# Cross-attention on one core: product 4 of the block product y in smaller blocks, sums of half 0 by accumulating DMA, result 12 evicted ahead of inner sums

## The chip, the cores and the metric

The kernel runs on one core of a Trainium2 chip. The metric is device time in microseconds (us) of one execution. A core has five engines with a queue of instructions each: PE (TensorE, matrix products into PSUM), DVE (VectorE), ACT (ScalarE), POOL (GpSimd) and SP (here a queue that issues DMAs). They meet through semaphores. Sixteen DMA engines move data; SP, ACT and POOL issue transfers to them.

## The reference

For each of 8 batches, with x1 and x2 of 512 x 1024 (channels x positions), in f32:

```python
q = jnp.einsum('bcn,dc->bnd', x1, Wq) + bq        # Wq: 64 x 512
k = jnp.einsum('bcn,dc->bdn', x2, Wk) + bk[:, None]
v = jnp.einsum('bcn,dc->bdn', x2, Wv) + bv[:, None]
attn = jax.nn.softmax(jnp.einsum('bnd,bdm->bnm', q, k), axis=2)
attn_out = jnp.einsum('bcm,bnm->bcn', v, attn)
return attn_out + x1
```

## The kernel before, in words

The values are never formed: the kernel computes y = x2 times the transposed attention (512 x 1024 by 1024 x 1024), scales it by one over the sums of the softmax, and then out = Wv y + bv + x1.

Both large products are done by a scheme of Strassen's kind with seven block products in place of eight (`MULT`: 1, 2, 6, 7, 5, 3, 4, in the order of their use). `first(i)` is block product i of y, `second(i)` that of the output. The left blocks of y are `a["11"]` to `a["22"]`, loaded from x2 transposed, and their sums S1 to S4; the right blocks are quarters of the exponentials `e` and their sums T1 to T4, all made on VectorE. The PSUM banks "a" and "c" (two of 128x512 each: j = 0, 1) are chains into which several block products accumulate; what has to leave a chain midway is copied by ScalarE to tiles `uy1`, `uy6`, `uy5` (tags u10 to u61). `evict_y` and `evict_o` combine a bank with such a copy on VectorE: result 11 of y is bank c after product 2 plus the copy from product 1, 22 is c after 7 plus the copy from 5, 12 is bank a after 3, 21 is c after 4 plus the copy from 6 (`RESULT`). Each result of y is then multiplied by `rden`, one over the softmax's sums.

A softmax half is 512 of the 1024 query positions (h = 0, 1), held as `e[h]` of 128 x 2 x 4 x 512. For each half: `scores` (PE) and copies to SBUF (ACT); `fold` and `fold_halves` of the maxima (DVE); `highest`, an all-reduce over the partitions (POOL); `exponentials`, a subtraction (DVE) and an exponential (ACT) for each of four slices; `sums`, three folds of 128x1024 and, in `total`, a fold of the two halves (DVE), an all-reduce (POOL) and a small DMA `few<-den`; `shares`, a reciprocal (DVE) and two DMAs on POOL's queue, `row<-few` to DRAM and the broadcast `den<-row` back.

`period(s, n, nn, nnn)` is the order of one batch s, written out by hand; nothing reorders it. It also makes the scores and exponentials of the next batch n, the queries of the one after it and loads. So every engine's queue is in the order of this program. Tiles come from pools with a tag and a number of buffers; a new tile waits until the old one of its buffer has been read.

Product 2 of y is already split once more, in batches 1 to 7: `inner_left` and `inner_right` make four sums each of the quarters of A12 and of the right block 21, `multiply_inner` issues seven products of 128x128 by 128x256 with two steps each, and `evict_inner` puts result 11 together on VectorE. In before, product 4 is one whole block product (`first(4)`: eight matmuls of 128x128 by 128x512); the sums of half 0 of the next batch are folded by VectorE just after the second scores, and `shares(n, 0)` follows the maxima of half 1.

An f32 matmul stands in the trace as two records.

Of the kernel before, what the change touches and what calls it, by code (L numbers as in the profile page):

```python
# [15 lines left out]
def kernel(  # L16
# [8 lines left out]
    bv: bass.AP,  # L25
    out: bass.AP,
):

# [187 lines left out]

    def total(s, h):
        fold_halves(s, h, ALU.add)  # L220
        s.den[h] = sb.tile([P, H], F32, tag="den", name=f"den_{s.b}_{h}", bufs=3)
        nc.gpsimd.partition_all_reduce(s.den[h], s.mx[h][:, 0, :], P, ReduceOp.add)  # L222
        s.few[h] = sb.tile([P, H // P], F32, tag="few", name=f"few_{s.b}_{h}", bufs=2)
        nc.gpsimd.dma_start(
            s.few[h], s.den[h][0:1, :].rearrange("o (p f) -> o p f", p=P)
        )
# [80 lines left out]
                s.tmp[i, j] = sb.tile([P, H], F32, tag=f"u{i}{j}", name=f"u{stage}{i}{j}_{s.b}")  # L307
                nc.scalar.copy(s.tmp[i, j], ps)  # L308

    def inner_left(s):  # L310

        x = s.a["12"]
        v = {
            f"{p + 1}{q + 1}": x[:, ts(q, MH // 2), ts(p, P)] for p in range(2) for q in range(2)
        }
        sums = sb.tile([P, 4, MH // 2, P], F32, tag="aS4", name=f"aI_{s.b}")
        for i, (k, x, y, op) in enumerate(
            (
                ("S1", "21", "22", ALU.add),
                ("S2", "S1", "11", ALU.subtract),  # L320
                ("S3", "11", "21", ALU.subtract),
                ("S4", "12", "S2", ALU.subtract),
            )
        ):
            v[k] = sums[:, i]
            nc.vector.tensor_tensor(v[k], v[x], v[y], op)
        s.inner["a"] = v

    def inner_right(s):

        x = s.e[0][:, 1]
        v = {
            f"{q + 1}{r + 1}": x[:, ts(q, MH // 2), ts(r, H // 2)]
            for q in range(2)
            for r in range(2)
        }
        sums = sb.tile([P, 4, MH // 2, H // 2], F32, tag="eT4", name=f"eI_{s.b}")
        for i, k in enumerate(("T1", "T2", "T3", "T4")):
            v[k] = sums[:, i]
            x, y = {"T1": ("12", "11"), "T2": ("22", "T1"), "T3": ("22", "12"), "T4": ("21", "T2")}[k]  # L340
            nc.vector.tensor_tensor(v[k], v[x], v[y], ALU.subtract)
        s.inner["t"] = v

    def multiply_inner(s):


        a, t = s.inner["a"], s.inner["t"]
        half = [P, H // 2]
        chain = ps_a.tile(half, F32, tag="c0", name=f"ps_i0_{s.b}")
        second = ps_a.tile(half, F32, tag="c1", name=f"ps_i1_{s.b}")  # L350
        third = ps_s.tile([P, 2, H], F32, tag="sc", name=f"ps_i2_{s.b}")[:, 0, 0 : H // 2]
        u = sb.tile([P, 2, H // 2], F32, tag="u50", name=f"i6_{s.b}")
        w = sb.tile([P, 2, H // 2], F32, tag="u51", name=f"i1_{s.b}")
        for i, ps, copy in (
            (1, chain, w[:, 0, :]),
            (2, second, None),
            (6, chain, u[:, 0, :]),
            (7, third, w[:, 1, :]),
            (5, chain, u[:, 1, :]),
            (4, third, None),  # L360
            (3, chain, None),
        ):
            ka, kb, _, _ = MULT[i]
            for k in range(MH // 2):
                nc.tensor.matmul(  # L365
                    ps,
                    a[ka][:, k, :],
                    t[kb][:, k, :],
                    start=i in (1, 2, 7) and k == 0,
                    stop=i in (2, 3, 4) and k == MH // 2 - 1,  # L370
                    skip_group_check=True,
                )
            if copy is not None:
                nc.scalar.copy(copy, ps)
        s.inner["ps"] = chain, second, third
        s.inner["u"] = u, w

    def evict_inner(s):

        chain, second, third = s.inner["ps"]  # L380
        u, w = s.inner["u"]
        u0, u1 = s.tmp[1, 0], s.tmp[1, 1]
        left, right = slice(0, H // 2), slice(H // 2, H)
        s.y["11"] = y = sb.tile([P, 2, H], F32, tag="y11", name=f"y11_{s.b}")
        for out, x, z in (
            (u0[:, left], u0[:, left], w[:, 0, :]),
            (y[:, 0, left], second, u0[:, left]),
            (u1, u1, u.rearrange("p a n -> p (a n)")),
            (y[:, 1, right], w[:, 1, :], u1[:, right]),
            (y[:, 1, left], third, u1[:, left]),  # L390
            (y[:, 0, right], chain, u0[:, right]),
        ):
            nc.vector.tensor_tensor(out, x, z, ALU.add)


    RESULT = {"11": ("c", 1), "22": ("c", 5), "12": ("a", None), "21": ("c", 6)}
# [26 lines left out]
    def evict_o(s, k):  # L423
        bank, add = RESULT[k]
        for j in range(2):
            c = 2 * (int(k[0]) - 1) + j
            o = s.o[k, j]
            nc.vector.scalar_tensor_tensor(  # L428
                o, s.bank[bank, j], bv_sb[:, c : c + 1], o, ALU.add, ALU.add
            )  # L430
        for j in range(2):
            c, h = 2 * (int(k[0]) - 1) + j, int(k[1]) - 1
            o = s.o[k, j]
            if add is not None:
                nc.vector.tensor_tensor(o, o, s.tmp[add, j], ALU.add)
            nc.sync.dma_start(out[s.b, ts(c, P), ts(h, H)], o)

    def sums(s, h):
        for i in range(1, MH):
# [95 lines left out]
    def period(s, n, nn, nnn):  # L535

        def first(i):
            multiply(s, "y", i, s.a, s.t, MH)  # L540

        def second(i):
            multiply(s, "o", i, w, s.y, 2)

        open_t(s)
        first(1)
        if s.b == 0:
            head_second(s, n)
        sum_e(s, "T1", "T2")
        if s.b == 0:  # L550
            total(s, 0)
        if n:
            load_a(n, "11")
        if s.b == 0:
            first(2)
            evict_y(s, "11", (1,))
            keys(n)
            load_x(nn, x1)
            sum_t4(s)
            sums(s, 1)  # L560
            shares(s, 0)
        else:
            multiply_inner(s)
            sums(s, 1)
            evict_inner(s)
            sum_t4(s)
            sum_a(s, "S4")
        sum_e(s, "T3")
        if n:
            load_a(n, "12", "21", "22")  # L570
        first(6)

        def next_queries():
            queries(nn)
            load_x(nn, x2)

        def next_keys():
            keys(nn)
            if nnn:
                load_x(nnn, x1)  # L580

        if n:
            scores_and(n, 0, "c", next_queries if nn else nothing)
            for i in range(1, MH):
                fold(n, 0, i, "max", ALU.max)
            highest(n, 0)
        shares(s, 1)
        evict_y(s, "11", (2,))
        first(5)
        fetch_o(s, "11")  # L590
        fetch_o(s, "22")
        if n:
            for i in range(MH):
                exponentials(n, 0, i)
            if s.b:
                sum_a(n, "S1", "S2", "S3")
        first(7)
        evict_y(s, "22")
        first(3)
        evict_y(s, "12")  # L600
        if n:
            scores_and(n, 1, "a", next_keys if nn else nothing)
            sums(n, 0)
        sum_y(s, "T1")
        sum_y(s, "T2")
        if n:
            if s.b:
                inner_left(n)
            else:
                left_sums(w, "S1", "S2", "S3", "S4")  # L610
            for i in range(1, MH):
                fold(n, 1, i, "max", ALU.max)
            highest(n, 1)
            shares(n, 0)
        first(4)
        evict_y(s, "21")
        second(1)
        sum_y(s, "T3")
        sum_y(s, "T4")
        second(6)  # L620
        fetch_o(s, "12")
        if n:
            exponentials(n, 1, 0)
            exponentials(n, 1, 1)
        second(2)
        evict_o(s, "11")
        fetch_o(s, "21")
        second(5)
        if n:
            exponentials(n, 1, 2)  # L630
            exponentials(n, 1, 3)
        second(7)
        evict_o(s, "22")
        if s.b == 0:
            sum_a(n, "S1", "S2")
        elif n:
            inner_right(n)
        if n:
            second(3)
            evict_o(s, "12")  # L640
            second(4)
            evict_o(s, "21")
            if s.b == 0:
                sum_a(n, "S3")
                inner_left(n)
                inner_right(n)
        else:
            second(4)
            evict_o(s, "21")
            second(3)  # L650
            evict_o(s, "12")
# [37 lines left out]
```

## Time and profile before

| what | value |
|---|---|
| median of 3 runs | 712.3 us (711.54 to 714.22) |
| the profiled execution | 711.94 us |
| its span, first to last instruction | 710.2 us |
| PE busy | 700.5 us, 1976 records |
| VectorE busy | 576.9 us |
| ScalarE busy | 210.7 us |
| POOL busy | 118.4 us |
| DMA moved | 91.67 MB, 129 GB/s on average |

A line of the page's groups reads: source line, engine, operation, tiles written and read, shape, count, then busy time in all, mean ns of one, and the idle time of the engine just before them with what ended it. A line of the timeline or of the chain begins with its start and its length in us. Engines are named PE, DVE, ACT, POOL; PEld is PE's load of weights.

### The profile page before, as it was taken

The page shows a single profiled execution, that of the slowest core. Times are in us where ns is not written, and L with a number is a line of the kernel's source. Part 1 is how long each engine was busy: PE and PEld are TensorE (multiplying, and loading weights), DVE is VectorE, ACT ScalarE, POOL GpSimd, SP SyncE. Part 2 cuts the span into 40 slices and gives each one's busy share as a digit, 9 for nine tenths or more (in the row PEclk, how much of TensorE's full clock was granted, in tenths as well). Part 3 has the DMA queues.
Part 4 walks back from the last instruction along what each step waited for, and adds up shares of the span by engine and source line. Part 5 has one row for each costly group of instructions (what it writes and reads, how often), then busy time and mean ns, then how long its engine had stood idle before and what let it go on. Part 6 is the DMA issues. An engine that isn't in the chain of part 4 may idle for free.

```text
span 710.2 us, 5772 instructions
## 1 busy us (share of the span) xinstructions
PE 700.5 (99%) x1976; PEld 315.8 (44%) x1976; DVE 576.9 (81%) x653; ACT 210.7 (30%) x299; POOL 118.4 (17%) x86
## 2 busy tenths in 40 slices
PE   8999999999999999999999999999999999999997
PEld 4333444534445434454344543454434544445443
DVE  0998698997989869888798887898788988999154
ACT  2733423144221522224221332413324134231010
POOL 0123130120402112021210212102121020402000
PEclk9999999999999999999999999999999999999999
DMA  9567333163431714327143362332702350042003
GB/s 327 221 227 255 111 148 134 60 198 99 161 121 61 257 37 163 149 82 244 37 147 128 119 208 90 123 128 89 237 0 74 119 178 16 5 167 80 15 0 148
DMA packets 37005, 91.67 MB, mean 129 GB/s; under 512 B 5232, under 2 KB 5232, under 8 KB 36976
## 3 DMA queue, kind: packets, MB, share of 16 engines
q1 hardware_dynamic: 33344, 84.95, 33.9%
q0 software_dynamic: 2368, 4.27, 2.8%
q10 hardware_dynamic: 1264, 2.10, 1.0%
q8 instruction: 15, 0.25, 0.2%
q14 instruction: 14, 0.11, 0.0%
HBM read 72.62 MB, written 16.81 MB: 126 GB/s over the span
## 4 chain that ended last, share of the span: by engine, by line
PE 85%; DVE 8%; DMA 4%; POOL 1%; issue 1%; ACT 1%; SPq 0%; DVEq 0%; ACTq 0%; POOLq 0%
PE ps_ya L298 25%; PE ps_oa L298 15%; PE ps_yc L298 15%; PE ps_oc L298 12%; PE ps_i L365 5%; PE ps_s L187 5%; PE ps_k L145 3%; PE ps_q L145 3%; DVE eT L251 2%; DMA x_head<-in_x_dram 1%; DVE e L245 1%; DMA row<-few 1%; PE ps_sa L187 1%; DVE sum L208 1%; DMA x_in_x_dram<-in_x_dram 1%; PE ps_sc L187 1%
## 5 line engine op out<-in xcount | busy, mean ns | idle before, releaser
L222 POOL PARTITION_ALL_REDUCE den<-sum x16 | 59.6, 3726 | 327.2 <-DVE sum L212 322.3
L298 PE MATMUL ps_ya<-eT,aS 128*128 128x512 f32 x256 | 113.1, 595 | 0.0
L308 ACT COPY uy<-ps_ya 128x512 f32<-128x512 f32 x48 | 28.0, 587 | 198.0 <-PE ps_ya L298 180.9
L298 PEld LDWEIGHTS ps_ya<-eT,aS 128*128 128x128 f32 x256 | 48.0, 190 | 60.9 <-issue 60.0
L245 DVE TENSOR_TENSOR e<-e,top 128x1024 f32<-128x1024 f32 x60 | 70.0, 1217 | 1.4 <-POOL top L217 1.4
L196 ACT COPY e<-ps_s 128x1024 f32<-128x1024 f32 x47 | 46.7, 1028 | 69.5 <-PE ps_s L187 67.2
L308 ACT COPY uo<-ps_oa 128x512 f32<-128x512 f32 x48 | 28.1, 585 | 130.7 <-PE ps_oa L298 129.2
L246 ACT ACTIVATE e<-e 128x1024 f32<-128x1024 f32 x60 | 61.0, 1052 | 19.2 <-DVE e L245 17.9
L298 PE MATMUL ps_yc<-e,a 128*128 128x512 f32 x144 | 63.4, 593 | 0.0
L428 DVE SCALAR_TENSOR_TENSOR o<-ps_oc,bv_sb,o 128x512 f32<-128x512 f32 x48 | 35.7, 747 | 29.3 <-PE ps_oc L298 29.0
L298 PE MATMUL ps_oc<-y,w 128*128 128x512 f32 x128 | 57.6, 593 | 0.0
L298 PE MATMUL ps_oa<-yT,w_S 128*128 128x512 f32 x128 | 57.5, 592 | 0.0
L298 PE MATMUL ps_ya<-e,a 128*128 128x512 f32 x128 | 56.3, 593 | 0.8 <-ACT e L240 0.8
L298 PE MATMUL ps_yc<-eT,a 128*128 128x512 f32 x128 | 57.0, 598 | 0.0
L217 POOL PARTITION_ALL_REDUCE top<-max x16 | 32.7, 2046 | 142.1 <-DVE few L230 87.9
L298 PE MATMUL ps_ya<-e,aS 128*128 128x512 f32 x128 | 56.2, 592 | 0.0
L187 PE MATMUL ps_s<-q,k 64*128 64x512 f32 x188 | 48.0, 609 | 2.8 <-ACT e L196 1.3
L298 PEld LDWEIGHTS ps_yc<-e,a 128*128 128x128 f32 x144 | 27.3, 190 | 34.8 <-issue 33.1
L208 DVE TENSOR_TENSOR max<-max,e 128x1024 f32<-128x1024 f32 x32 | 39.2, 1225 | 3.7 <-ACT e L194 0.5
L412 DVE TENSOR_TENSOR y<-ps_yc,uy 128x512 f32<-128x512 f32 x34 | 22.3, 679 | 24.4 <-PE ps_yc L298 24.4
L414 DVE TENSOR_TENSOR y<-y,den 128x512 f32<-128x512 f32 x48 | 35.7, 785 | 6.4 <-DMA den<-row 6.4
L208 DVE TENSOR_TENSOR sum<-sum,e 128x1024 f32<-128x1024 f32 x32 | 39.2, 1225 | 2.1
(85 smaller groups left out, 897.2 us busy)
## 6 DMA issues: line engine op xcount, KB each, us to landing
x_in_x_dram<-in_x_dram SPq DMA_DIRECT2D x56, 512.0 KB, 6.0
a<-in_x2T_dram SPq DMA_DIRECT2D x32, 512.0 KB, 4.6
o<-in_x_dram SPq DMA_DIRECT2D x64, 256.0 KB, 6.2
out_dram<-o SPq DMA_DIRECT2D x64, 256.0 KB, 2.0
x_head<-in_x_dram SPq DMA_DIRECT2D x8, 512.0 KB, 8.3
den<-row POOLq DMA_DIRECT2D x16, 256.0 KB, 3.6
q<-q ACTq DMA_DIRECT2D x14, 128.0 KB, 7.3
w<-in_wvT_dram SPq DMA_DIRECT2D x4, 256.0 KB, 8.9
```

The costliest lines, as they stand in the source:

```text
L145: nc.tensor.matmul(ps[r, :], w_sb[:, c, :], s.x[:, c, ts(h, H)], start=(c == 0), stop=(c == CT - 1),)
L187: nc.tensor.matmul(ps[g], s.k[r, ts(i, P)], s.q[r, ts(h, H)], start=True, stop=True)
L196: nc.scalar.copy(e[:, :, i, :], whole)
L208: nc.vector.tensor_tensor(f, e[:, :, 0, :] if i == 1 else f, new, op)
L222: nc.gpsimd.partition_all_reduce(s.den[h], s.mx[h][:, 0, :], P, ReduceOp.add)
L245: nc.vector.tensor_tensor(e, e, top, ALU.subtract)
L246: nc.scalar.activation(e, e, AF.Exp)
L298: nc.tensor.matmul(ps, left[ka][:, k, ts(j, P)], right[kb][:, k, :], start=opens and k == 0, stop=i in (2, 3, 4) and k == n_k - 1, skip_gr ...
L308: nc.scalar.copy(s.tmp[i, j], ps)
L365: nc.tensor.matmul(ps, a[ka][:, k, :], t[kb][:, k, :], start=i in (1, 2, 7) and k == 0, stop=i in (2, 3, 4) and k == MH // 2 - 1, skip_gro ...
L414: nc.vector.tensor_tensor(y[:, j, :], y[:, j, :], rden, ALU.mult)
L428: nc.vector.scalar_tensor_tensor(o, s.bank[bank, j], bv_sb[:, c : c + 1], o, ALU.add, ALU.add)
```

## The change

It changes five things.

1. Product 4 of y is split into seven half-width products in batches 1 to 7, as product 2 is (`multiply_4`). The sums of A22's quarters are made by `inner_left` into a tile of tag a12, those of T4's by `inner_right` into one of tag eT2. Three of the pieces accumulate straight into bank c; two chains stand in the PSUM buffers of tag sc. ScalarE makes five copies, and `add_copies` brings them into the copy of product 6 by three additions on VectorE.
2. The sum over half 0 of the next batch is no longer folded on VectorE: ScalarE copies slice 0 to the tile, and three DMAs issued by POOL add the other slices into it (`start_sum`, after the exponentials). `total` of it follows the maxima of half 1, in batch 0 the eviction of 21; `shares` of it goes to the next batch, after T1 and T2.
3. The scaling of result 11 goes from ahead of `first(5)` to behind `first(7)`. In batch 1 the sums of half 1 go behind T4 and S4.
4. At the batch's end the sums for product 2 move: `inner_left` stands behind the eviction of output 22, and output 12 leaves PSUM ahead of `inner_right`.
5. A12 of the next batch is loaded after product 4, apart from A21 and A22; tag den has two buffers for three.

The diff, cut to its core (`inner_left`, `inner_right` and the former `multiply_inner` and `evict_inner`, now `multiply_2`, keep their work for product 2):

```diff
-        s.den[h] = sb.tile([P, H], F32, tag="den", name=f"den_{s.b}_{h}", bufs=3)
+        s.den[h] = sb.tile([P, H], F32, tag="den", name=f"den_{s.b}_{h}", bufs=2)
...
+    def inner_product(s, i, z, ps, opens, *copies):
+        ka, kb, _, _ = MULT[z]
+        for k in range(MH // 2):
+            nc.tensor.matmul(
+                ps,
+                s.inner[i][ka][:, k, :],
+                s.inner[i, "t"][kb][:, k, :],
+                start=opens and k == 0,
+                stop=z in (2, 3, 4) and k == MH // 2 - 1,
+                skip_group_check=True,
+            )
+        for copy in copies:
+            nc.scalar.copy(copy, ps)
...
+    def inner_bank(s, i, z):
+        return ps_s.tile([P, 2, H], F32, tag="sc", name=f"ps_i{i}{z}_{s.b}")[:, 0, left]
...
+    def multiply_4(s):
+        c0, c1 = s.bank["c", 0], s.bank["c", 1]
+        chain, third = inner_bank(s, 4, 0), inner_bank(s, 4, 2)
+        d = [sb.tile([P, 2, H // 2], F32, tag=f"u5{j}", name=f"i4{j}_{s.b}") for j in range(2)]
+        v = sb.tile([P, H // 2], F32, tag="u10", name=f"i47_{s.b}")
+        for z, ps, opens, *copies in (
+            (1, chain, True, d[0][:, 0, :]),
+            (7, third, True, v),
+            (6, chain, False, d[1][:, 0, :]),
+            (2, c0[:, left], False),
+            (5, chain, False, d[0][:, 1, :], d[1][:, 1, :]),
+            (4, c1[:, left], False),
+            (3, c0[:, right], False),
         ):
-            nc.vector.tensor_tensor(out, x, z, ALU.add)
+            inner_product(s, 4, z, ps, opens, *copies)
+        def add_copies():
+            both = v.unsqueeze(1).to_broadcast([P, 2, H // 2])
+            nc.vector.tensor_tensor(d[1], d[1], both, ALU.add)
+            for j in range(2):
+                u6 = s.tmp[6, j]
+                nc.vector.tensor_tensor(u6, u6, d[j].rearrange("p a n -> p (a n)"), ALU.add)
+        return add_copies
...
+    def start_sum(s, h):
+        e = s.e[h]
+        s.mx[h] = f = sb.tile([P, 2, H], F32, tag="fold", name=f"sum_{s.b}_{h}", bufs=2)
+        nc.scalar.copy(f, e[:, :, 0, :])
+        for i in range(1, MH):
+            nc.gpsimd.dma_start(f, e[:, :, i, :], accum_op=ALU.add)
...
         sum_e(s, "T1", "T2")
         if s.b == 0:
             total(s, 0)
+        else:
+            shares(s, 0)
...
         else:
-            multiply_inner(s)
-            sums(s, 1)
-            evict_inner(s)
+            evict = multiply_2(s)
+            if s.b > 1:
+                sums(s, 1)
+            evict()
             sum_t4(s)
             sum_a(s, "S4")
+            if s.b == 1:
+                sums(s, 1)
         sum_e(s, "T3")
         if n:
-            load_a(n, "12", "21", "22")
+            load_a(n, "21", "22")
         first(6)
+        if s.b:
+            inner_right(s, 4, s.t["T4"], "eT2")
...
         shares(s, 1)
-        evict_y(s, "11", (2,))
         first(5)
         fetch_o(s, "11")
         fetch_o(s, "22")
         if n:
             for i in range(MH):
                 exponentials(n, 0, i)
+            start_sum(n, 0)
             if s.b:
                 sum_a(n, "S1", "S2", "S3")
         first(7)
+        if s.b > 1:
+            inner_left(s, 4, s.a["22"], "a12")
+        evict_y(s, "11", (2,))
         evict_y(s, "22")
         first(3)
         evict_y(s, "12")
+        if s.b == 1:
+            inner_left(s, 4, s.a["22"], "a12")
         if n:
             scores_and(n, 1, "a", next_keys if nn else nothing)
-            sums(n, 0)
         sum_y(s, "T1")
         sum_y(s, "T2")
         if n:
-            if s.b:
-                inner_left(n)
-            else:
+            if s.b == 0:
                 left_sums(w, "S1", "S2", "S3", "S4")
             for i in range(1, MH):
                 fold(n, 1, i, "max", ALU.max)
             highest(n, 1)
-            shares(n, 0)
-        first(4)
+            if s.b:
+                total(n, 0)
+        if s.b:
+            multiply_4(s)()
+        else:
+            first(4)
+        if n:
+            load_a(n, "12")
         evict_y(s, "21")
+        if s.b == 0:
+            total(n, 0)
         second(1)
...
         second(7)
         evict_o(s, "22")
-        if s.b == 0:
-            sum_a(n, "S1", "S2")
-        elif n:
-            inner_right(n)
         if n:
+            if s.b:
+                inner_left(n, 2, n.a["12"], "aS4")
+            else:
+                sum_a(n, "S1")
             second(3)
             evict_o(s, "12")
+            if s.b:
+                inner_right(n, 2, n.e[0][:, 1], "eT4")
+            else:
+                sum_a(n, "S2")
             second(4)
             evict_o(s, "21")
             if s.b == 0:
                 sum_a(n, "S3")
-                inner_left(n)
-                inner_right(n)
+                inner_left(n, 2, n.a["12"], "aS4")
+                inner_right(n, 2, n.e[0][:, 1], "eT4")
```

More of the change, by code (lines that the diff above doesn't have):

```diff
@@ L308, in multiply, with inner_left @@
                 nc.scalar.copy(s.tmp[i, j], ps)
-    def inner_left(s):
-        x = s.a["12"]
+    LEFT = (
+        ("S1", "21", "22", ALU.add),
+        ("S2", "S1", "11", ALU.subtract),
+        ("S3", "11", "21", ALU.subtract),
+        ("S4", "12", "S2", ALU.subtract),
+    )
+    RIGHT = (
+        ("T1", "12", "11", ALU.subtract),
+        ("T2", "22", "T1", ALU.subtract),
+        ("T3", "22", "12", ALU.subtract),
+        ("T4", "21", "T2", ALU.subtract),
+    )
+    def inner_left(s, i, x, tag):
+        v = {f"{p + 1}{q + 1}": x[:, ts(q, MH // 2), ts(p, P)] for p in range(2) for q in range(2)}
+        sums = sb.tile([P, 4, MH // 2, P], F32, tag=tag, name=f"aI{i}_{s.b}")
+        for z, (k, x, y, op) in enumerate(LEFT):
+            v[k] = sums[:, z]
+            nc.vector.tensor_tensor(v[k], v[x], v[y], op)
+        s.inner[i] = v
@@ L313, in inner_left, with inner_right @@
+    def inner_right(s, i, x, tag):
         v = {
-            f"{p + 1}{q + 1}": x[:, ts(q, MH // 2), ts(p, P)] for p in range(2) for q in range(2)
+            f"{q + 1}{r + 1}": x[:, ts(q, MH // 2), ts(r, H // 2)] for q in range(2) for r in range(2)
         }
[L316 to L322, printed above, removed]
-            )
-        ):
-            v[k] = sums[:, i]
-            nc.vector.tensor_tensor(v[k], v[x], v[y], op)
@@ L327, in inner_left @@
[L327 to L361, printed above, removed]
-        ):
[L363 to L393, printed above, removed]
+        sums = sb.tile([P, 4, MH // 2, H // 2], F32, tag=tag, name=f"eI{i}_{s.b}")
@@ new lines, in inner_right @@
+        for z, (k, x, y, op) in enumerate(RIGHT):
+            v[k] = sums[:, z]
+            nc.vector.tensor_tensor(v[k], v[x], v[y], op)
+        s.inner[i, "t"] = v
+    def inner_product(s, i, z, ps, opens, *copies):
[8 more added lines that the diff above has]
+                skip_group_check=True,
+            )
+        for copy in copies:
+            nc.scalar.copy(copy, ps)
@@ new lines, with multiply_2, evict @@
+    left, right = slice(0, H // 2), slice(H // 2, H)
+    def inner_bank(s, i, z):
+        return ps_s.tile([P, 2, H], F32, tag="sc", name=f"ps_i{i}{z}_{s.b}")[:, 0, left]
+    def multiply_2(s):
+        chain = ps_a.tile([P, H // 2], F32, tag="c0", name=f"ps_i20_{s.b}")
+        second = ps_a.tile([P, H // 2], F32, tag="c1", name=f"ps_i21_{s.b}")
+        third = inner_bank(s, 2, 2)
+        u = sb.tile([P, 2, H // 2], F32, tag="u50", name=f"i26_{s.b}")
+        v = sb.tile([P, 2, H // 2], F32, tag="u51", name=f"i21_{s.b}")
+        for z, ps, opens, *copies in (
+            (1, chain, True, v[:, 0, :]),
+            (2, second, True),
+            (6, chain, False, u[:, 0, :]),
+            (7, third, True, v[:, 1, :]),
+            (5, chain, False, u[:, 1, :]),
+            (4, third, False),
+            (3, chain, False),
+        ):
+            inner_product(s, 2, z, ps, opens, *copies)
+        def evict():
+            u0, u1 = s.tmp[1, 0], s.tmp[1, 1]
+            s.y["11"] = y = sb.tile([P, 2, H], F32, tag="y11", name=f"y11_{s.b}")
+            for out, x, z in (
+                (u0[:, left], u0[:, left], v[:, 0, :]),
+                (y[:, 0, left], second, u0[:, left]),
+                (u1, u1, u.rearrange("p a n -> p (a n)")),
+                (y[:, 1, right], v[:, 1, :], u1[:, right]),
+                (y[:, 1, left], third, u1[:, left]),
+                (y[:, 0, right], chain, u0[:, right]),
+            ):
+                nc.vector.tensor_tensor(out, x, z, ALU.add)
+        return evict
@@ new lines, in multiply_4 @@
+    def multiply_4(s):
[3 more added lines that the diff above has]
+        v = sb.tile([P, H // 2], F32, tag="u10", name=f"i47_{s.b}")
+        for z, ps, opens, *copies in (
+            (1, chain, True, d[0][:, 0, :]),
[5 more added lines that the diff above has]
+            (3, c0[:, right], False),
+        ):
+            inner_product(s, 4, z, ps, opens, *copies)
[6 more added lines that the diff above has]
+        return add_copies
```

## The prediction, made before the changed kernel had run

> **What bounds the kernel now.** I read the page first, then the chain that ended last, then one middle batch engine by engine, then the few places where PE waits, then the DMA share in 2-us stretches.
>
> ```profile
> span 710.2 us, 5772 instructions
> ...
> PE 700.5 (99%) x1976; PEld 315.8 (44%) x1976; DVE 576.9 (81%) x653; ACT 210.7 (30%) x299; POOL 118.4 (17%) x86
> ```
>
> PE is busy 700.5 of 710.2 us at the full granted clock (the PEclk row is 9 throughout). VectorE is next with 81%, but the queue that matters is PE's. The chain, cut to one batch (batch 3, from 297.08 to 383.19):
>
> ```profile
> 297.08 6.87 PE ps_ya L298 x16
> 303.95 6.04 PE ps_i L365 x28
> ...
> 344.88 1.92 PE ps_s L187 x8
> ...
> 348.51 3.58 PE ps_k L145 x16
> 352.10 7.06 PE ps_yc L298 x16
> 359.16 6.87 PE ps_oa L298 x16
> ...
> 383.19 0.86 PE ps_ya L298 x2
> ```
>
> All of it is PE without a gap: a batch costs 86.11 us, and only PE work taken out shortens it. The second and fifth printed rows are the two kinds of block product. Product 2 runs as seven half-width pieces (28 records, two for each f32 matmul) in 6.04 us; product 4 is still whole (16 records), 6.87 us plus 0.19 because it follows the 64-row key matmuls.
>
> Two places in the first batches, where PE does wait:
>
> ```profile
> 86.08 1.29 PE L187 MATMUL ps_sa<-q,k 64*128 64x512 f32 x3
> ...
> 147.15 1.13 PE L187 MATMUL ps_s<-q,k 64*128 64x512 f32 x4 [1.26 <-ACT e L196]
> ```
>
> ```profile
> 85.34 1.28 DVE L410 TENSOR_TENSOR y<-ps_ya,den 128x512 f32<-128x512 f32 x2
> ```
>
> ```profile
> 146.09 1.93 ACT L196 COPY e<-ps_s 128x1024 f32<-128x1024 f32 x2 [2.35 <-DVE eT L251]
> ```
>
> In batch 0 the scores start at 83.95 and the keys at 88.59, 4.64 us; in batch 3 the same stretch is 344.88 to 348.51, 3.63. The 1.0 us is VectorE emptying bank a late (85.34). In batch 1, ScalarE may not overwrite e before VectorE has read it for T4, and PE loses 1.26.
>
> **The change, part by part.** Times t count from the batch's start (297.08 for batch 3).
>
> *PE.* In batches 1 to 7 product 4 becomes 28 half-width records: 6.87 to 6.04, so -0.83 each, 7 x 0.83 = -5.8. The order of the pieces leaves one whole piece (0.86) between a piece and the next on its bank; product 2 keeps that distance and shows no gap. New is that the second piece opens the PSUM buffer that the keys used: their ScalarE eviction ran 0.69 from t = 55.06 to 55.75, the piece may start at 55.02 + 0.19 + 0.86 = 56.07. I cost it at 0 to 0.3 a batch, take 0.05, 0.3 in all.
>
> *VectorE, per batch.* These rows give the prices:
>
> ```profile
> L208 DVE TENSOR_TENSOR sum<-sum,e 128x1024 f32<-128x1024 f32 x32 | 39.2, 1225 | 2.1
> ...
> L341 DVE TENSOR_TENSOR eI<-e 128x512 f32<-128x512 f32 x14 | 9.6, 684 | 0.0
> ...
> L326 DVE TENSOR_TENSOR aI<-a 128x256 f32<-128x256 f32 x14 | 5.8, 415 | 0.0
> ```
>
> Added: four sums of A22's quarters 4 x 0.415 = 1.7, four of T4's 4 x 0.685 = 2.7, three additions of the copies 3 x 0.69 = 2.1: 6.5. Removed: three folds of half 0's sum, 3 x 1.225 = 3.7. Net +2.8 on 72.5, so 75.3 in a batch of 85.3: it still fits on average. In place: T4's sums go where VectorE idled 1.93 us before the maxima (317.95 to 319.95), so the maxima of half 0 start some 2 us later. With the later end of the batch before (the 2.7 of inner_right now stands ahead of result 21's eviction) I get them done at t = 29.5 instead of 27.4, and the first exponential's subtraction at about 33. ScalarE is not free for it before 34.7 (its L308 copy at 331.18 ends there), so the exponentials still end at t = 38.6. After that the removed folds put VectorE ahead: the maxima of half 1 end at 55.3 instead of 63.3.
>
> *ScalarE.* Five copies of 0.372 and one of 1.03 on 26.1 us: hidden, it idles 10.29 us before the second scores. The copy that seeds the sum ends at t = 39.7.
>
> *POOL and the accumulating DMAs* decide the case. Half 0's sum is now three transfers of 512 KB, SBUF to SBUF, each issued by POOL only when the one before has landed. The joining fold waits for the third, on VectorE's queue; behind it stand the additions of the copies, result 21's eviction, T3 and T4. Their cover: from t = 40 on, POOL has nothing to do until the maxima of half 1, and the DMA engines are empty:
>
> ```profile
> 335.10:337.10 2.00, 0.00 (x0) 1.00 0.79 252
> ...
> 341.10:343.10 2.00, 0.00 (x0) 1.00 0.00 0
> ...
> 351.10:353.10 2.00, 2.00 (x1) 1.00 0.00 0
> 353.10:355.10 2.00, 1.71 (x2) 1.00 1.00 328
> ```
>
> (the last two columns are DMA share and GB/s). They stay empty until t = 56; then the next x load fills them to t = 64. The last moment: the additions read a tile (tag u10) that ScalarE must overwrite with its first copy of second(1), and second(6) on PE needs that copy by t = 64.7. Copy 0.58, addition 0.69, join 0.69 and hand-overs bring the landing to t = 62.6 at the latest: 22.6 us for three.
>
> What one costs, no row shows. Nearest is den<-row, also issued by POOL, 256 KB:
>
> ```profile
> DMA to landing us min/median/max: 3.3/3.6/6.3
> ```
>
> A 2-KB one (few<-den) takes 1.9. So 256 KB add 1.4 and 512 KB 2.8: 4.7 us if bytes count once. The lower end is 1.9 + 512 KB at the loads' 350 GB/s = 3.4; the upper end counts the bytes twice, because the destination is read as well: 1.9 + 5.6 = 7.5. [...] I take 5.5, nearer to the row: landing at 40 + 16.5 = 56.5, six us early. Cost 0.
>
> [...] POOL's all-reduce of that sum moves to about t = 58 to 62, beside the additions, which read two SBUF operands.
>
> ```profile
> 309.02 2.20 DVE L393 TENSOR_TENSOR uy<-uy,i 128x512 f32<-128x512 f32 x1
> ```
>
> That addition took 2.20 instead of 0.69 beside an all-reduce (308.34 to 311.67). [...]
>
> *Moves with no price.* shares of half 0 go to the next batch, after T1 and T2: POOL's row and den DMAs (0.56, 0.54) and the wait for the row's landing (up to 8 us) now stand ahead of half 1's sum; its reciprocal comes at t = 29.6, cover 10 us. den loses a buffer; the sum of the new half 0 takes the one of the old half 1, read last at t = 48.5. A12's load goes behind product 4 (t = 61.3), with SP's fetch of o12 behind it; they are wanted at about t = 80, after landings of 4.6 and 6.2. y11's scaling goes from before the exponentials to after: nothing needs it before t = 48.5.
>
> *Batches 0 and 1.* In batch 0 y11's scaling waited until 77.19 for den and held the exponentials at 78.40, though the maxima were there at 75.85. Without it bank a is empty some 1 us earlier: the 1.0 us goes. In batch 1 half 1's sum (4.4) moves behind T4, so T4 ends at about 140.5, before the scores at 143: the 1.26 goes. Next to be late there are half 1's scores, with over 2 us of slack. Ends 0 and -2.3, I take -2.2.
>
> *Sum:* -5.8 - 2.2 + 0.3 = -7.7. The profiled execution took 711.94 for its span of 710.2, so 704.2; the median of the runs is 0.4 above it, so 704.6.
>
> **The rivals.**
> *The sums land late (slower).* Place: the join on VectorE. If one transfer takes 7 us, the third starts at 54, meets the x load from 56, and lands near 64, 1.4 us late in each of six batches: +8, all is eaten. At 8 us it lands near 68, 5 us late: +30, so 735. It decides from about 6.8 us a transfer. For it: the upper end of 7.5 is past that. Against: 1.4 us for 256 KB already contains a slow rate. 716 to 745.
> *VectorE becomes the bound.* [...] If each batch loses 0.6 to 1 us of PE at second(2) or second(6), the gain is gone: 708 to 714. Against: slack of 1 us or more everywhere I looked.
> *Product 4 does not get its 0.83.* If pieces wait for the keys' eviction or the copies by 0.3 to 0.5: 706.5 to 708.5. Against: product 2 has no such gap.
>
> **How the numbers follow.** Forecast 0.70 (702 to 706.5), late sums 0.16, VectorE 0.07, product 4 short 0.07. A measurement here tells about 0.5%, 3.6 us, from no change. Faster beyond it (below 708.7): 0.70 + 0.07 + 0.01 = 0.78; same 0.06; slower 0.16. The range 701.5 to 712 takes in the forecast, product 4 and most of VectorE's case, 0.82.
>
> **What would show it.** Right: product 4's slot 28 records in 6.0 to 6.3, a batch of 85.3, no PE wait of 1 us near 86 and 147, the join waiting less than 3 us for the DMA at t near 55, landings of about 5.5. Wrong: the join waiting past t = 62, ScalarE's first uo copy waiting for VectorE, PE idle ahead of second(6) or second(2), or a batch at 86 or more.

## The result, and the profile after

The changed kernel takes 705.09 us (median of 4 runs, 704.42 to 706.35) against 712.09 in the same comparison: a ratio of 0.9898, with a 95% interval of 0.9874 to 0.9923. The forecast was 704.6, with a range of 701.5 to 712. The profiled execution took 705.11 for a span of 703.3.

The page:

```profile
PE 693.5 (99%) x2060; PEld 331.1 (47%) x2060; DVE 581.0 (83%) x709; ACT 229.2 (33%) x341; POOL 138.8 (20%) x107
```

PE is still the bound and is busy 7.0 us less, in 84 records more. VectorE is busy 4.1 us more over the whole kernel, ScalarE 18.5, POOL 20.4.

The chain that ended last, cut to batch 3 (start, length, what):

```profile
294.21 6.87 PE ps_ya L300 x16
301.08 6.04 PE ps_i L349 x28
...
345.64 3.58 PE ps_k L147 x16
349.23 2.79 PE ps_i L349 x12
352.01 0.86 PE ps_yc L349 x4
352.88 0.86 PE ps_i L349 x4
353.74 1.73 PE ps_yc L349 x8
355.47 6.87 PE ps_oa L300 x16
...
379.50 6.87 PE ps_ya L300 x16
```

The batch lasts 379.50 - 294.21 = 85.29 (before 86.11). Product 4 is the four rows from 349.23 to 355.47, 6.24 us in 28 records: 6.04 and the 0.19 behind the key matmuls. No piece waited.

The accumulating DMAs in batch 3, on POOL's timeline (start, length of the issue, engine, line, operation; in brackets the idle time before and who ended it), and for all 21 the time from issue to landing:

```profile
334.05 1.25 POOL L476 DMA_DIRECT2D sum<-e  x1 [1.86 <-ACT sum L474]
339.42 1.20 POOL L476 DMA_DIRECT2D sum<-e  x1 [4.13 <-DMA sum<-e]
344.73 1.17 POOL L476 DMA_DIRECT2D sum<-e  x1 [4.11 <-DMA sum<-e]
```

```profile
DMA to landing us min/median/max: 5.0/5.0/12.1
```

One transfer took 5.0 us, so the third landed at about 349.7, t = 55.5 of the batch. VectorE's join and the additions:

```profile
349.74 0.69 DVE L214 TENSOR_TENSOR sum<-sum 128x512 f32<-128x512 f32 x1
354.45 0.69 DVE L419 TENSOR_TENSOR i<-i,i 128x512 f32<-128x512 f32 x1 [4.02 <-ACT i L358]
355.06 1.29 DVE L422 TENSOR_TENSOR uy<-uy,i 128x512 f32<-128x512 f32 x2
```

The join waited for nothing; VectorE then stood idle 4.02 us until the copies of product 4 were there. The longest landing, 12.1, is batch 0's third, and there PE waited:

```profile
92.96 1.17 POOL L476 DMA_DIRECT2D sum<-e  x1 [4.15 <-DMA sum<-e]
```

```profile
105.08 0.69 DVE L214 TENSOR_TENSOR sum<-sum 128x512 f32<-128x512 f32 x1 [4.95 <-DMA sum<-e]
```

```profile
106.83 3.26 DVE L253 TENSOR_TENSOR yT<-y,yT 128x1024 f32<-128x1024 f32 x1
```

```profile
113.08 3.70 PE L300 MATMUL ps_oc<-y,w 128*128 128x512 f32 x8 [1.14 <-DVE o L459]
```

The late transfer is not the only cause. Behind the join VectorE makes a sum for the output (`yT`) that takes 1.22 us where it runs alone (344.03, batch 3); here it took 3.26, beside POOL's all-reduce of the sum (105.87 to 110.00). These 2.0 us are more than PE's 1.14, so by this trace PE waited for the two delays together.

By batches, from the starts of `first(1)` in the two traces (us; negative is shorter after):

| stretch | before | after | difference |
|---|---|---|---|
| head and batch 0 | 123.3 | 123.6 | +0.3 |
| batch 1 | 87.65 | 85.29 | -2.4 |
| batches 2 to 5, each | 86.11 | 85.29 | -0.82 |
| batch 6 | 79.10 | 78.69 | -0.4 |
| batch 7 to the end | 75.69 | 74.54 | -1.15 |

The sum is -6.9, the difference of the spans.

### The profile page after: what moved, and what is told of

Its sections match the earlier page's. It is cut to its first block, busy times and chain, and to the rows that moved or that the text cites. A ratio compares the mean times of both kernels' runs of the same rounds, so it can differ in the third digit from the quotient of the medians.

```text
span 703.3 us, 6098 instructions
## 1 busy us (share of the span) xinstructions
PE 693.5 (99%) x2060; PEld 331.1 (47%) x2060; DVE 581.0 (83%) x709; ACT 229.2 (33%) x341; POOL 138.8 (20%) x107
## 3 DMA queue, kind: packets, MB, share of 16 engines
q0 software_dynamic: 8080, 15.28, 11.8%
## 4 chain that ended last, share of the span: by engine, by line
PE 83%; DMA 7%; DVE 5%; POOL 2%; ACT 1%; issue 1%; SPq 0%; POOLq 0%; ACTq 0%; DVEq 0%
PE ps_ya L300 28%; PE ps_oa L300 14%; PE ps_oc L300 11%; PE ps_i L349 10%; PE ps_yc L300 7%; PE ps_s L189 4%; DMA sum<-e 3%; PE ps_yc L349 3%; PE ps_k L147 3%; PE ps_q L147 3%; DMA a<-in_x2T_dram 1%; DMA row<-few 1%; POOL den L224 1%; DVE eT L253 1%; DMA w<-in_wvT_dram 1%
## 5 line engine op out<-in xcount | busy, mean ns | idle before, releaser
L224 POOL PARTITION_ALL_REDUCE den<-sum x16 | 55.1, 3441 | 34.2 <-DVE sum L214 29.1
L234 POOL DMA_DIRECT2D row<-few x16 | 9.1, 567 | 215.8 <-DVE few L232 190.6
L253 DVE TENSOR_TENSOR eT<-e,eT 128x1024 f32<-128x1024 f32 x32 | 48.4, 1532 | 0.5
L476 POOL DMA_DIRECT2D sum<-e x21 | 25.3, 1204 | 76.3 <-DMA sum<-e 58.5
L349 PE MATMUL ps_i<-eI,aI 128*128 128x256 f32 x168 | 39.8, 380 | 0.2 <-ACT e L198 0.2
```

What stands on the lines that cost most here:

```text
L253: nc.vector.tensor_tensor(t[k], t[x], t[y], ALU.subtract)
L349: nc.tensor.matmul(ps, s.inner[i][ka][:, k, :], s.inner[i, "t"][kb][:, k, :], start=opens and k == 0, stop=z in (2, 3, 4) and k == MH // 2 ...
```

## The experiments

The first four ran on one chip, with before at 711.96; the next four on another, with before at 711.76; the last two on a third, at 711.54. A difference across these groups carries up to 0.4 us of that. Each kernel is the changed one with the edit shown, unless its heading names another.

**The changed kernel again.** 

> The changed kernel again, beside the others on the same chip: 704.4 to 706.4 us, as in its first runs. A batch of 85.3 us.

Measured: 704.41 us (704.07 to 705.34), ratio 0.9902 (0.9887 to 0.9917). Its profile shows a batch of 85.29 and, unlike the one above, no wait of PE in batch 0: there the third transfer was issued 0.67 us earlier and took 11.6 us, and the join waited 3.59; VectorE's sum behind it took 3.27. So that wait comes and goes with 1.2 us in the landing.

**Product 4 whole again.**

```diff
-        if s.b:
-            inner_right(s, 4, s.t["T4"], "eT2")
...
-            inner_left(s, 4, s.a["22"], "a12")
...
-        if s.b:
-            multiply_4(s)()
-        else:
-            first(4)
+        first(4)
```

> Product 4 of y whole again in all batches; the accumulating DMAs and all moves stay. Theory (the gain is PE work): a batch back at 86.1 us, 0.83 us more in batches 1 to 5 and 7, 0.4 in batch 6 (where the split pieces wait for score copies): 5.4 us more than the changed kernel, 710.5. Rival (the gain comes from VectorE's queue, which is relieved by the DMA sums): product 4 matters little, at most 1 us more, 706; VectorE then has 6.5 us less in a batch, so it might even be faster.

Measured: 709.49 us, ratio 0.9967 (0.9956 to 0.9978). 5.1 us more than the changed kernel. The chain of batch 3:

```profile
294.92 6.87 PE ps_ya L300 x16
...
349.93 7.06 PE ps_yc L300 x16
...
381.03 4.29 PE ps_ya L300 x10
```

86.11 again. The rival is out: VectorE is busy 66.56 us in batch 3 instead of 72.21 in the changed kernel beside it, and the kernel is slower, by PE's own work. Batch 6 went from 78.70 to 78.94 only: there the split keeps 0.24 of its 0.83. The sum is 5 x 0.83 + 0.24 + 0.8 = 5.2.

**All sums of half 0 on VectorE.**

```diff
-            start_sum(n, 0)
...
             highest(n, 1)
+            for i in range(1, MH):
+                fold(n, 0, i, "sum", ALU.add)
             if s.b:
                 total(n, 0)
```

> No accumulating DMAs: the three folds of half 0's sum are VectorE's again, but stand behind the maxima of half 1, where VectorE idled 4.02 us in batch 3. Theory (the DMAs are covered and not needed for the gain): a middle batch stays at 85.3; PE's 1.14 us wait in batch 0, behind the third transfer of 12.1 us, goes: 704.0, within 703.5 to 705. Rival (VectorE, 83% busy, can't carry product 4's sums and these folds together): second(2) or second(6) waits in each batch, 1 us or more, 711 or more.

Measured: 706.5 us, ratio 0.9927 (0.9914 to 0.9939). Neither. Batches 1 to 5 are 85.3 as the theory has it, and batch 0 has no wait; but batch 6 takes 81.2 instead of 78.7. On its PE and ScalarE timelines:

```profile
608.34 3.70 PE L300 MATMUL ps_oa<-yT,w_S 128*128 128x512 f32 x8 [1.29 <-ACT uo L310]
612.80 3.67 PE L300 MATMUL ps_oc<-y,w 128*128 128x512 f32 x8 [0.77 <-DVE y L445]
```

```profile
607.70 1.07 ACT L310 COPY uo<-ps_oa 128x512 f32<-128x512 f32 x2 [5.13 <-DVE i L419]
```

Batch 6 has no queries and no keys to make (7.2 us of PE), while VectorE's work is the same. There VectorE is the bound, busy 78.1 of 81.2 us: the additions come late, ScalarE's first uo copy waits 5.13 us for the tile that they read, and PE waits for it: the deadline of the prediction, reached from another side. The two additions into the copy of product 6 then took 3.33 us instead of 1.29, beside POOL's all-reduce (607.10 to 610.70), ahead of PE's second wait of 0.77.

**Batch 0's sum alone on VectorE.**

```diff
-            start_sum(n, 0)
+            if s.b:
+                start_sum(n, 0)
...
             highest(n, 1)
+            if s.b == 0:
+                for i in range(1, MH):
+                    fold(n, 0, i, "sum", ALU.add)
```

> Only batch 0's sum of the next half 0 goes back to VectorE's folds, behind the maxima of half 1; batches 1 to 6 keep the DMAs. Theory (the third transfer met the x load at 93 us and held the join, then the exponentials, then output 11's eviction and PE): PE's wait at 113 goes, 1.1 us less than the changed kernel, 704.0. Rival (PE in batch 0 waits for VectorE's work as such): three folds more on VectorE make it the same or up to 1 us longer.

Measured: 703.75 us (703.54 to 703.85), ratio 0.9888 (0.9874 to 0.9901). 0.7 less than the changed kernel beside it and with a narrower spread: the wait is there in one of the two traces of the changed kernel, so its median may show a part of it. The intervals of the two ratios overlap; the direction rests on the runs, which do not, and on the trace that has the wait. This kernel's trace has none. Nor has the second trace of the changed kernel, with VectorE's sum at 3.27 us beside the all-reduce (104.67 to 108.81): that meeting alone did not make PE wait.

**Batch 1 in the old order.**

```diff
-            if s.b > 1:
-                sums(s, 1)
+            sums(s, 1)
             evict()
...
-            if s.b == 1:
-                sums(s, 1)
```

> In batch 1 the sums of half 1 stand ahead of the eviction of result 11 again, as in batches 2 to 7. Theory (that order alone let T4 end after the next scores in batch 1, so that ScalarE, and then PE, waited): PE's wait at the first scores of batch 1 is back, 1.3 us more than the changed kernel, 705.7. Rival (batch 1 waited because batch 0 had left VectorE late, which the other moves cure): no wait, 704.4.

Measured: 705.91 us, ratio 0.992 (0.9906 to 0.9934), 1.5 more than the changed kernel's 704.41, on another chip; the intervals of the two ratios overlap a little. The trace has the wait back, with the same causes one behind the other:

```profile
145.39 1.93 ACT L198 COPY e<-ps_s 128x1024 f32<-128x1024 f32 x2 [2.52 <-DVE eT L253]
```

```profile
146.45 1.13 PE L189 MATMUL ps_s<-q,k 64*128 64x512 f32 x4 [1.43 <-ACT e L198]
```

Part of it is an addition of result 11's eviction, ahead of T4: 2.13 us of the chain from 139.79, where it takes 0.68 in batch 1 of the changed kernel. In before, in the same order, it took 2.20 at 140.41, beside POOL's all-reduce (139.72 to 143.05).

**The sums five microseconds later.**

```diff
-        nc.scalar.copy(f, e[:, :, 0, :])
+        nc.vector.tensor_copy(f, e[:, :, 0, :])
...
-            start_sum(n, 0)
...
         evict_y(s, "22")
+        if n:
+            start_sum(n, 0)
         first(3)
```

> The sum's seed is copied by VectorE behind the eviction of result 22 instead of by ScalarE, so the first accumulating DMA starts about 5 us later (t = 45 instead of 39.8 of a batch). Theory (deadline at t = 62.6; a third transfer issued beside the x load takes 12.1 instead of 5.0 us): the third is issued at t = 55.8, lands near 68, ScalarE's first uo copy waits for VectorE and PE for it, about 5 us in each of batches 0 to 6: 739, within 725 to 745. Rival (the cover is not tight, VectorE's order absorbs 5 us): under 710.

Measured: 751.16 us (one run), 47 us more than the changed kernel and outside what was expected. The mechanism is the one named, in batches 1 to 4. In batch 3 the third transfer was issued at 370.79, 57 us into the batch, met the x load, and the join waited 12.67 us; then the chain of waits runs through ScalarE to PE:

```profile
381.86 0.69 DVE L214 TENSOR_TENSOR sum<-sum 128x512 f32<-128x512 f32 x1 [12.67 <-DMA sum<-e]
```

```profile
383.88 6.68 PE L300 MATMUL ps_oa<-yT,w_S 128*128 128x512 f32 x8 [5.57 <-ACT uo L310]
```

The size was off for a second reason, in the same row: eight records took 6.68 us instead of 3.60. The stretches of the trace (PE busy and records, granted clock, DMA share, GB/s) say why:

```profile
378.00:379.00 1.00, 0.31 (x1) 1.00 1.09 254
...
382.00:383.00 1.00, 0.00 (x0) 1.00 0.27 104
...
384.00:385.00 1.00, 1.00 (x2) 0.50 0.00 0
...
390.00:391.00 1.00, 1.00 (x4) 1.00 0.00 0
```

PE's granted clock fell from 1.00 to 0.50 4.8 us after its last record, and was back at 1.00 6.0 us after PE resumed. Over the kernel PE waited 30.9 us for these ScalarE copies, in batches 1 to 4 and 6, and the slow records behind them add 12.0 (6.68, 6.23, 5.98, 5.92 and 5.22 instead of 3.60 each). Batch 5, whose third transfer meets no x load, lost 0.4. Batch 6 has no x load either, and its third transfer took 5.1 us; PE waited 6.76 all the same, as without query and key matmuls it had come to second(6) 58.7 us into the batch, in batch 5 after 64.5.

**A copy in place of the accumulation.**

```diff
-            nc.gpsimd.dma_start(f, e[:, :, i, :], accum_op=ALU.add)
+            nc.gpsimd.dma_start(f, e[:, :, i, :])
```

> The three DMAs copy instead of accumulate, so the sum of half 0 leaves out three slices; all waits stay. Theory (an accumulating transfer reads its destination too, and that doubles its data time): 3.4 to 3.8 us from issue to landing against 5.0, and half of the engine time. Rival (the price is that of 512 KB from POOL's queue in any case): 5.0 again. The time is that of the changed kernel, 703.5 to 705.5, by both, since the DMAs are covered; batch 0's wait gets shorter.

Measured: 703.6 us (one run), and all 21 transfers:

```profile
L476 POOL DMA_DIRECT2D sum<-e x21: 704/712/726, 82.0 to 593.7; - x21
...
DMA to landing us min/median/max: 3.1/3.1/3.4
```

3.1 us against 5.0. Of the 1.9 us of difference 0.5 lies in the issue on POOL (0.71 against 1.20) and the rest in the transfer. The 16 engines' time for POOL's queue fell from 11.8% of the span to 6.6%; 2.8% is what it had in before, without these transfers. In batch 3 the second accumulating transfer had 0.60 of the 16 engines for 5.08 us, 3.0 us of all of them, the second copy 1.4. So an accumulating transfer held the engines more than twice as long as a copy. That fits the theory; that it is the reading of the destination which costs, no run shows by itself. The expected 3.4 to 3.8 was a little high. The third in batch 0 was issued 2.2 us ahead of the x load (88.79 and 90.95), and none of the 21 took more than 3.4.

**Result 11 of batch 0 scaled early again**, on top of the kernel with batch 0's sum on VectorE.

```diff
         shares(s, 1)
+        if s.b == 0:
+            evict_y(s, "11", (2,))
         first(5)
...
-        evict_y(s, "11", (2,))
+        if s.b:
+            evict_y(s, "11", (2,))
```

> On top of e3_b0_dve (703.75), result 11 of batch 0 is scaled ahead of first(5) again. Theory (its wait for den held the exponentials and so the eviction of result 12 from bank a): PE waits at the second scores of batch 0 again, 1.0 us more than e3_b0_dve, 704.8. Rival (that wait came from VectorE's three folds, which stood behind it): no more than 0.3 us, 704.

Measured: 704.52 us, ratio 0.99 (0.9887 to 0.9914), 0.8 more than without the edit by the medians, but the intervals overlap. In its trace the exponentials start at 77.67, behind the wait for den, and the stretch from scores to keys is 83.78 to 87.85, 4.07 us where its parent has 3.64. That is the theory's direction with 0.4 to 0.8 of its 1.0; den was there at 76.45 in this execution, 0.7 earlier than in before, so the wait was shorter.

**Batch 0's sum on VectorE and another order of pieces in batch 6.**

```diff
-        for z, ps, opens, *copies in (
...
+        for z in (1, 2, 6, 7, 5, 4, 3) if s.b == B - 2 else (1, 7, 6, 2, 5, 4, 3):
+            ps, opens, *copies = pieces[z]
```

> e3_b0_dve (703.75), and in batch 6 alone the half-width pieces of product 4 in the order 1, 2, 6, 7, 5, 4, 3 (before 1, 7, 6, 2, 5, 4, 3), so that the piece that waits for the last score copy comes two pieces later. Theory (batch 6 has no key matmuls ahead of product 4, and its second piece waits for ScalarE, 0.4 us in all): 0.2 to 0.4 less than e3_b0_dve, 703.4. Rival (the wait moves to the third piece, whose copy stands behind the same score copies on ScalarE): the same, 703.75.

Measured: 703.48 us (703.23 to 703.7), ratio 0.9885 (0.9869 to 0.9902). Batch 6 is 78.20 instead of 78.68, and its trace shows no wait of PE after the head. This is the fastest kernel here, 0.3 below its parent by the medians, which the intervals don't separate.

**Accumulating DMAs in batch 6 alone.**

```diff
-            start_sum(n, 0)
+            if s.b == B - 2:
+                start_sum(n, 0)
...
+            if s.b < B - 2:
+                for i in range(1, MH):
+                    fold(n, 0, i, "sum", ALU.add)
```

> The sums of half 0 on VectorE in batches 0 to 5 (as in e2_dve_sums, behind the maxima), by accumulating DMAs in batch 6 alone. Theory (the DMAs buy time only in batch 6, where there are no query and key matmuls and so 7.2 us less cover for VectorE; elsewhere the folds fit a hole): the 2.5 us that e2_dve_sums lost are back, 703.7 as e3_b0_dve. Rival (with the folds on VectorE it is late in every batch and the loss only shows at the end): 706.

Measured: 703.96 us, ratio 0.9891 (0.9877 to 0.9906), as the theory said: the 2.5 us that batch 6 lost with the folds are back, and batches 1 to 5 do not care which engine sums. The accumulating DMAs thus earn their place in batch 6 alone.

No run undoes the moves at the batch's end, the separate load of A12 or the smaller den pool; what each of them is worth by itself stays open.

## Why the prediction was right, step by step

*PE's work, -5.8 and 0.3 of waits.* Right in kind and close in size: 5.1 with product 4 alone undone. The middle batches gave 0.82 each, without a wait. What the step missed is batch 6. It costed the second piece's wait for the keys' eviction at 0.05 a batch; in batch 6 there are no keys, the buffer is that of the last scores, and their copy ends just then:

```profile
599.26 1.99 PE L349 MATMUL ps_i<-eI,aI 128*128 128x256 f32 x8 [0.22 <-ACT e L198]
```

Batch 6 gained 0.4 instead of 0.83, 0.24 of it by the split, and the other order of pieces brought 0.48 more.

*VectorE's net +2.8, cover enough.* Right in the cover, wrong in the sum. VectorE was busy 71.78 us in batch 3 after 72.48, so 0.7 less, and 4.1 us more over the kernel, where 7 x 2.8 is 19.6. The count of instructions was right; what it left out is where they meet POOL's all-reduces. In batch 3 before, VectorE instructions beside three all-reduces took 1.5, 0.8 and 1.9 us more (2.20 instead of 0.69; two in 2.10 instead of 1.28; 3.15 instead of 1.22); after, one such meeting is left, with 1.5 (two sums in 3.87 instead of 2.35). The prediction did not count on fewer of them, so part of the cover was luck. In place, the half 0 maxima ended at t = 29.0 (29.5 said), the exponentials at 38.6 (38.6), the half 1 maxima at 55.6 (55.3). The rival that VectorE becomes the bound did not come true in the changed kernel; with all folds put back it decides batch 6, and no other.

*The accumulating DMAs, 5.5 each, landing at t = 56.5.* 5.0 and 55.5. The value is close, but by two errors that offset each other. A plain copy of 512 KB took 3.1, so the 4.7 that came from the row of den<-row was 1.6 too high for bytes counted once. The accumulation then added 1.9, for which 5.5 leaves 0.8. That the one made up for the other was luck.

*Deadline at t = 62.6 and what a miss costs.* The place was right (the uo copy, then second(6)). The price was too low: the rival's 735 for 5 us late leaves out the clock. The granted clock stayed at 1.00 through a wait of 1.43 us (batch 1 in the old order) and one of 1.89 (the late sums, batch 0), and was 0.50 after one of 5.57. In three of the five waits of the late sums it fell 2.5 us (batch 1), 4.5 (batch 6) and 4.8 (batch 3) after the end of PE's last record, and came back 4.5, 4.6 and 6.0 us after PE resumed. The runs show no one length of wait for it.

*POOL's all-reduce beside the additions, nothing in the sum.* Right for batch 3, and there without the 1.5 us that the row showed (2.20 instead of 0.69): the all-reduce of the sum ran from 351.98 to 355.29, while VectorE stood idle for ScalarE's copies until 354.45. The first addition then began with 0.84 us of the all-reduce left and still took 0.69, the other two 1.29. In batches 1 and 6 the additions were longer: in batch 1 the first one, begun 0.25 us into the all-reduce, took 2.54 instead of 0.69, in batch 6, where the join waited 1.89 us, two additions 3.33 instead of 1.29. These 1.9 and 2.0 us, of all-reduces of 3.23 and 3.60, are above the row's 1.5, and PE did not wait for them. In batch 0, where the step did not look, 2.0 us of the same kind stand in the chain to PE's wait of 1.14.

*Batches 0 and 1, -2.2.* This step failed in part. Batch 1's 1.26 came, for the reason given, and a little more: the batch was 1.54 us longer than a middle one before and is as long as one after. With the order undone 1.5 came back. Batch 0's 1.0 came at the scores (keys at 87.49 instead of 88.59) and was given back 25 us later, in the profiled execution as a wait of 1.14: the working had placed the deadline in the middle batches and did not do it for batch 0. In batch 3 the first transfer was issued 15.2 us ahead of the x load (334.05 and 349.26), in batch 0 only 8.9 (82.29 and 91.18). There the third transfer was issued at 92.96, 1.8 us behind the load, and took 12.1. The rival of the late sums was thus true in one batch, in the execution first profiled.

The sum said -7.7, the spans -6.9. Of the difference of 0.8, batch 0 makes +1.2 (it ended 0.3 later, not 0.9 earlier) and batch 6 +0.4; against them stand batch 1 with -0.3, the kernel's end with -0.4, of which 0.3 is a last store that landed sooner, and the middle batches with -0.1. That the total came so near owes something to these offsets; its main term, PE's work, does not.

## What to carry to other kernels

When one engine is busy 99% of the time, count its work first; a step that moves work to others is then worth what it lets that engine drop, and each of its covers has to be checked in every batch that differs: the first (here a load nearer to the transfer) and the last but one (no queries and keys to hide under) decided what the middle did not show. A count of instructions is not yet a price: an instruction can cost more where it meets another engine's (here 3.26 us instead of 1.22 for an addition beside an all-reduce), and a move can remove or create such a meeting. A chain of dependent transfers is costed by its last one, which may start beside a load and take more than twice as long (here 12.1 us instead of 5.0). And a stall that starves the matrix engine for some microseconds can cost more than its own length (here 5.57 us of wait and 3.1 more in the slow records behind it).

## What the runs showed of the hardware

- An accumulating transfer of 512 KB from SBUF to SBUF on POOL's queue: 1.20 us to issue and 5.0 to landing, against 0.71 and 3.1 for a plain copy; issued 1 to 2 us behind a 2 MB load, 11.6 and 12.1 us.
- These issues took 1168 to 1250 ns over all 21; in batch 3 1.20 us with VectorE idle (339.42), 1.25 and 1.17 with VectorE busy (334.05 and 344.73).
- Additions on VectorE that began beside a partition all-reduce of a sum on POOL: 2.54 us instead of 0.69 (0.25 us into it, after, batch 1), 2.20 instead of 0.69 (0.68 into it, before, batch 3), 3.26 instead of 1.22 (0.96 into it, after, batch 0), 3.15 instead of 1.22 (1.06 into it, before, batch 3); 0.69 for one that began with 0.84 us of the all-reduce left (after, batch 3). All-reduces are timed here as the profile gives them.
- In the run with the late sums PE's granted clock halved 2.5 us (batch 1), 4.5 (batch 6) and 4.8 (batch 3) after PE's last record, and stayed there for 4.5 to 6.0 us of work; it stayed at 1.00 through waits of 1.43 us (batch 1 in the old order) and 1.89 (the late sums, batch 0).
